# A linear attention with experts: the k times v products of a pair of heads formed on 32 columns of the array, behind the products of scores and v

## The chip, the cores and the metric

The kernel runs on one core of one Trainium2 chip. The metric is the time of one execution in microseconds (us) on the device; where a profile is shown, its span is the time from the first to the last instruction of the profiled execution. The engines are TensorE (PE, with the load of its stationary operand shown as PEld), VectorE (DVE), ScalarE (ACT), GpSimd (POOL) and SyncE (SP, which issues transfers here).

## The reference

The input x has 8 sequences of 1024 tokens with 256 features, all in fp32. A layer norm is followed by two branches whose results are added to x. The first is a causal linear attention with 16 heads of 16 features; the second sends each token to 2 of 8 experts.

```python
xn = layernorm(x)
# attention, per head (d, e run over 16 features)
q = elu(xn @ Wq.T) + 1;  k = elu(xn @ Wk.T) + 1;  v = xn @ Wv.T
kv_cumsum = cumsum(einsum('blhd,blhe->blhde', k, v), axis=1)
k_cumsum = cumsum(k, axis=1)
out = einsum('blhd,blhde->blhe', q, kv_cumsum)
out = out / clip(einsum('blhd,blhd->blh', q, k_cumsum), 1e-06, None)
attn = out @ Wo.T
# experts: the best 2 of 8, softmax over the two
h = silu(xn @ W1[e]) * (xn @ W3[e]);  y_e = h @ W2[e]
result = x + attn + sum(weight_e * y_e)
```

## The kernel before

The tokens are cut into 16 blocks of 512 (two per sequence), and a block into 4 chunks of 128, so there are 64 chunks. The experts' work is cut into tiles of 128 tokens that go to the same expert; 132 of them run. A loop over the expert tiles is the frame: each turn does one expert tile (`ffn_step`: two groups of 16 records gu, the gate and the up product, L1216; the turn of the next tile's tokens, L1183; the down product y of the tile before, L1235), and one or two steps of the attention are put between the turns by `attend_upto`. A block of the attention has nine steps: four for its projections (`project`), one for the scores of its first chunk, and four that weigh one chunk each. The instructions are not written out in their final order: a scheduler sets it on each engine, from the program's order, the dependencies and its own costs. From before to after it places the surrounding work anew.

The attention runs chunk by chunk. For a chunk, causality within it is taken by masked scores, and everything ahead of it by a state, one 16 x 16 matrix per head, which is the sum of k times v over all earlier chunks of the sequence.

- `scores(t, c)`: eight products (L919) on 32 rows of the array each, one row strip for each r, write q times k for 16 heads to four PSUM tiles `s_ps`, which are all four buffers of the pool `ps_mm`; the experts' products gu take their two from the same pool. VectorE multiplies each tile with the causal mask (L926) into `s_sb`, of the pool `masked` with seven buffers: four for the chunk that waits to be weighed, three for the next. Then two products (L934), one for each half of the 16 heads (`KC` = 2), form k times v: the stationary operand is 128 columns of k (8 heads), the moving one the 128 columns of v of these heads. Of the 128 x 128 result only the eight blocks of 16 x 16 on the diagonal are wanted; VectorE multiplies by a mask of them (`heads_b`, L939), and adds the state so far (L941), unless the chunk is the first of its sequence. The last chunk of a sequence needs no k times v.
- `weigh(t, c)`: two products of the state with q (L953; left out in the first chunk of a sequence), then sixteen of v and scores (L960) which each make 32 rows of the output on 32 columns of the array, all summed in the PSUM tile `o_ps`. VectorE multiplies with the reciprocal of the denominator (L967) to `oT`.
- `attend(t, c, oT)`: the two products with Wo (L979), copied by ScalarE and added to the output.

`block_steps` calls `scores` one chunk ahead of `weigh`, and `attend` one chunk behind it. Each fp32 product shows as two records in the trace: a group of 4 records is 2 products, 32 records are 16 products. The layout of v, `va`, holds pairs of heads: for each pair, one block of 32 columns with the first head's v and zeros, and one with zeros and the second's; `own_v` picks the filled 16 of each. `kv_ps`, `o_ps`, the turned tokens `xg_t` and the transposes `tp` share the pool `ps_t` with two buffers.

Of the kernel before, what the change touches and what calls it, by code (L numbers as in the profile page):

```python
# [46 lines left out]
F32 = mybir.dt.float32  # L47
# [3 lines left out]
ALU = mybir.AluOpType  # L51
AX = mybir.AxisListType

P = 128
# [3 lines left out]
PAIR = 2 * HD  # L58
# [5 lines left out]
def tile_attention_moe(  # L64
# [14 lines left out]
    nc = tc.nc  # L79
    B, L, H = x.shape  # L80
    E, _, I = w1.shape
    KC = H // P
    IC = I // P
    TB = 512
    NCH = TB // P
    N = B * L
    NBLK = N // TB
    BLK_PER_SEQ = L // TB
# [22 lines left out]
    three = ctx.enter_context(tc.tile_pool(name="three", bufs=3))  # L111
# [3 lines left out]
    ps_t = ctx.enter_context(tc.tile_pool(name="ps_t", bufs=2, space=bass.MemoryType.PSUM))  # L115
# [114 lines left out]
    heads = const.tile([P, P], F32, name="heads")  # L230
# [16 lines left out]
    va = const.tile([P, NCH, HALF, 2, PAIR], F32, name="va")  # L247
# [12 lines left out]
        nc.gpsimd.tensor_copy(own_of[:, o, o * HALF : (o + 1) * HALF], own)  # L260

    causal_b = causal.unsqueeze(1).to_broadcast([P, 4, P])
    heads_b = heads.unsqueeze(1).to_broadcast([P, KC, P])


    lgs = {}
# [116 lines left out]
    new = f_one.tile([P, E, MOST], F32, name="new")  # L383
# [384 lines left out]
    def own_v(va, c, a, b):  # L768

        pairs = va[:, c, a:b].rearrange("p g s d -> p g (s d)")  # L770
        return pairs.rearrange("p g (q d) -> p g q d", d=HD)[:, :, 0:4:3, :]
# [135 lines left out]
    state = [None]  # L907

    def scores(t, c):

        qT, qm, kT, kn, va, rden = blocks[t]
        first = t % BLK_PER_SEQ == 0 and c == 0
        last = t % BLK_PER_SEQ == BLK_PER_SEQ - 1 and c == NCH - 1
        span = bass.ts(c, P)
        s_ps = [ps_mm.tile([P, KC, 2, P], F32, tag="mm", name="s_ps") for r in range(4)]
        for hh in range(KC):
            for r in range(4):
                rows = slice(32 * r, 32 * r + 32)
                nc.tensor.matmul(  # L919
                    s_ps[r][:, hh].rearrange("p a l -> p (a l)"), lhsT=kT[rows, hh, span],  # L920
                    rhs=qm[rows, hh, :, span], start=True, stop=True,
                )
        s_sb = []
        for r in range(4):
            sm = masked.tile([P, KC * 2, P], F32, tag="s_sb", name="s_sb")
            nc.vector.tensor_tensor(  # L926
                sm, s_ps[r].rearrange("p k a l -> p (k a) l"), causal_b, ALU.mult
            )
            s_sb.append(sm)
        before_c = state[0]  # L930
        if not last:
            kv_ps = ps_t.tile([P, KC, P], F32, tag="t", name="kv_ps")
            for hh in range(KC):
                nc.tensor.matmul(  # L934
                    kv_ps[:, hh, :], lhsT=kn[:, c, bass.ts(hh, P)],
                    rhs=own_v(va, c, 4 * hh, 4 * hh + 4), start=True, stop=True,
                )
            new = three.tile([P, KC, P], F32, tag="kv", name="kv")
            nc.vector.tensor_tensor(new, kv_ps, heads_b, ALU.mult)  # L939
            if not first:  # L940
                nc.vector.tensor_tensor(new, new, before_c, ALU.add)  # L941
            state[0] = new
        return t, c, s_sb, before_c

    def weigh(t, c, s_sb, before_c):

        qT, qm, kT, kn, va, rden = blocks[t]
        first = t % BLK_PER_SEQ == 0 and c == 0
        span = bass.ts(c, P)
        o_ps = ps_t.tile([P, KC, P], F32, tag="t", name="o_ps")  # L950
        if not first:
            for hh in range(KC):
                nc.tensor.matmul(  # L953
                    o_ps[:, hh, :], lhsT=before_c[:, hh, :], rhs=qT[:, hh, span],
                    start=(hh == 0), stop=False, skip_group_check=True,
                )
        for hh in range(KC):
            for a in range(2):
                for r in range(4):
                    nc.tensor.matmul(  # L960
                        o_ps[32 * r : 32 * r + 32, hh, :],
                        lhsT=va[:, c, 4 * hh + r, a, :],
                        rhs=s_sb[r][:, 2 * hh + a, :],
                        start=(first and a == 0), stop=(a == 1), skip_group_check=True,
                    )
        oT = two.tile([P, KC, P], F32, tag="oT", name="oT")
        nc.vector.tensor_tensor(oT, rden[:, c], o_ps, ALU.mult)  # L967
        return oT

    ats = {}  # L970
# [24 lines left out]
    def block_steps(t):  # L995


        for i, _ in enumerate(project(t)):
            if i == 1 and behind:
                attend(*behind.pop())  # L1000
            if i in (1, 3, 5, 8):
                yield
        if t + 1 < NBLK:
            fetch(t + 1)
        waiting = scores(t, 0)
        yield
        done = None
        for c in range(NCH):
            coming = scores(t, c + 1) if c + 1 < NCH else None
            if done and c + 1 < NCH:  # L1010
                attend(*done)
            oT = weigh(*waiting)
            if done and c + 1 == NCH:
                attend(*done)
            done = t, c, oT
            waiting = coming
            if c + 1 < NCH or t + 1 < NBLK:
                yield
        behind.append(done)
        if t + 1 == NBLK:  # L1020
            attend(*behind.pop())
            yield
# [24 lines left out]
    with tc.manual_schedule(engines={EN.DVE, EN.Activation, EN.PE, EN.Pool}):  # L1047
# [63 lines left out]
        for _ in range(2):  # L1111
            idle_ps = ps_mm.tile([P, TB], F32, tag="mm", name="idle_ps")
            nc.tensor.matmul(
                idle_ps, lhsT=ident, rhs=blocks[0][0][:, 0, :], start=True, stop=True
# [170 lines left out]
    for j in range(NM + 1):  # L1285
        if j + 1 < NM:
            ffn_norm(j + 1)
        t = FB + j
# [27 lines left out]
        if LISTS <= j < LISTS + NBLK - FB:  # L1316
            t = FB + j - LISTS
# [66 lines left out]
```

## Time and profile before

| | |
|---|---|
| time, median of 3 runs | 1318.28 us (1317.63 to 1319.15) |
| the profiled execution: its time, its span | 1329.68 us, 1328.0 us |
| granted TensorE clock, mean | 0.989 |
| TensorE: gate and up products L1216 | 4224 records, 511.2 us busy |
| TensorE: down product L1235 | 1056 records, 250.6 us |
| TensorE: scores L919 | 1024 records, 85.5 us |
| TensorE: scores times v L960 | 2048 records, 73.2 us |
| TensorE: state times q L953 | 224 records, 34.9 us |
| VectorE: masked scores L926 | 256 instructions of 128x512, mean 684 ns |
| VectorE: k times v masked L939, state added L941 | 56 of mean 417 ns, 48 of mean 426 ns |
| VectorE: `oT` L967 | 64 of mean 414 ns |

A line of groups gives the source line, the engine, the operation, the tiles it writes and reads, the shapes and the count; then the busy time in us, the mean of one in ns, and the idle time of the engine ahead of it. A line of the timeline gives the start and the width in us, the engine, the source line and the count of instructions of that group which followed each other. A matmul's shape is given by its stationary operand (rows*columns) and its moving one.

### The profile page before, as it was taken

The page shows a single profiled execution, that of the slowest core. Times are in us where ns is not written, and L with a number is a line of the kernel's source. Part 1 is how long each engine was busy: PE and PEld are TensorE (multiplying, and loading weights), DVE is VectorE, ACT ScalarE, POOL GpSimd, SP SyncE. Part 2 cuts the span into 40 slices and gives each one's busy share as a digit, 9 for nine tenths or more (in the row PEclk, how much of TensorE's full clock was granted, in tenths as well). Part 3 has the DMA queues.
Part 4 walks back from the last instruction along what each step waited for, and adds up shares of the span by engine and source line. Part 5 has one row for each costly group of instructions (what it writes and reads, how often), then busy time and mean ns, then how long its engine had stood idle before and what let it go on. Part 6 is the DMA issues. An engine that isn't in the chain of part 4 may idle for free.

```text
span 1328.0 us, 28290 instructions
## 1 busy us (share of the span) xinstructions
PE 1270.6 (96%) x10968; PEld 1092.2 (82%) x10968; DVE 636.9 (48%) x1436; ACT 526.1 (40%) x1060; POOL 523.1 (39%) x460
## 2 busy tenths in 40 slices
PE   5689999999999999999999999999999999999996
PEld 4478887787888888888888888898888888888886
DVE  7667489764252434435343535344443525243441
ACT  4466364461524325161525243341515152433411
POOL 3633333233254443443443525343434334343432
PEclk9899999999999999999999999999999999999998
DMA  9688576466685766666675757476676767575763
GB/s 340 229 276 258 154 200 170 130 173 206 176 229 141 198 166 155 189 173 172 169 190 145 216 132 208 126 188 171 160 186 170 189 153 194 147 198 134 198 161 72
DMA packets 163462, 240.36 MB, mean 181 GB/s; under 512 B 16098, under 2 KB 87394, under 8 KB 163042
## 3 DMA queue, kind: packets, MB, share of 16 engines
q1 hardware_dynamic: 119938, 184.31, 45.0%
q0 software_dynamic: 38064, 43.22, 19.3%
q10 hardware_dynamic: 5328, 11.01, 2.3%
q8 instruction: 90, 1.47, 0.5%
q14 instruction: 42, 0.34, 0.1%
HBM read 196.30 MB, written 52.67 MB: 187 GB/s over the span
## 4 chain that ended last, share of the span: by engine, by line
PE 87%; DVE 7%; ACT 2%; issue 1%; DMA 1%; another core or an unknown queue 1%; POOL 0%; POOLq 0%; DVEq 0%; ACTq 0%
PE gu_ps L1216 34%; PE y_ps L1235 16%; PE o_ps L960 5%; PE s_ps L919 5%; PE a_ps L979 4%; PE zq L795 4%; PE zkk L811 4%; PE zkv L811 4%; PE kv_ps L934 2%; PE o_ps L953 2%; PE xg_t L1183 2%; DVE s_sb L926 1%; PE tp L333 1%; PE den L880 1%; PE tp L858 1%
## 5 line engine op out<-in xcount | busy, mean ns | idle before, releaser
L1216 PE MATMUL gu_ps<-xgT,w 128*128 128x128 f32 x4224 | 511.2, 278 | 8.9 <-DVE s_sb L926 7.6
L1216 PEld LDWEIGHTS gu_ps<-xgT,w 128*128 128x128 f32 x4224 | 492.5, 193 | 28.8 <-issue 12.5
L1162 POOL DMA_INDIRECT xg<-in_x_dram,src_i x132 | 128.1, 970 | 406.1 <-ACT xgT L1185 322.4
L1246 POOL DMA_INDIRECT out_dram<-y,dst_i x107 | 176.3, 1648 | 222.2 <-DVE kn L765 54.2
L1235 PE MATMUL y_ps<-w_sb,hT 128*128 x1056 | 250.6, 380 | 2.6 <-DVE hT L1227 2.0
L1227 DVE TENSOR_TENSOR hT<-gu_ps,hT 128x512 f32<-128x512 f32 x132 | 91.1, 690 | 274.4 <-PE gu_ps L1216 198.0
L1235 PEld LDWEIGHTS y_ps<-w_sb,hT 128*128 128x128 f32 x1056 | 190.2, 190 | 24.0 <-DVE hT L1227 1.9
L1224 ACT ACTIVATE hT<-gu_ps 128x512 f32<-128x512 f32 x132 | 78.8, 597 | 299.9 <-PE gu_ps L1216 255.0
L926 DVE TENSOR_TENSOR s_sb<-s_ps,causal 128x512 f32<-128x512 f32 x256 | 163.6, 684 | 54.0 <-PE s_ps L919 25.5
L1242 DVE TENSOR_SCALAR y<-y_ps,entry 128x256 f32<-128x256 f32 x132 | 63.5, 481 | 120.0 <-PE y_ps L1235 75.0
L1167 POOL DMA_INDIRECT entry<-tab_d,of_i x107 | 106.5, 995 | 32.6 <-issue 30.5
L1185 ACT COPY xgT<-xg_t 128x256 f32<-128x256 f32 x132 | 49.0, 371 | 145.2 <-PE xg_t L1183 141.7
L984 ACT COPY at<-a_ps 128x256 f32<-128x256 f32 x64 | 23.7, 370 | 159.2 <-PE a_ps L979 149.0
L919 PE MATMUL s_ps<-qm,kT 32*128 32x256 f32 x1024 | 85.5, 405 | 0.5 <-DVE hT L1227 0.4
L1174 ACT ACTIVATE xg<-xg,entry 128x256 f32<-128x256 f32 x132 | 79.6, 603 | 3.4 <-issue 3.4
L960 PE MATMUL o_ps<-s_sb,va 128*32 128x128 f32 x2048 | 73.2, 276 | 0.0
L919 PEld LDWEIGHTS s_ps<-qm,kT 32*128 32x128 f32 x1024 | 51.0, 184 | 24.2 <-issue 19.6
L979 PE MATMUL a_ps<-wo_sb,oT 128*128 128x256 f32 x256 | 69.0, 393 | 0.1
L1246 POOL DMA_INDIRECT acc_d<-y,src_i x25 | 44.0, 1761 | 55.2 <-DVE y L1242 15.4
L960 PEld LDWEIGHTS o_ps<-s_sb,va 128*32 128x32 f32 x2048 | 53.2, 109 | 9.8 <-DVE oT L967 0.8
L811 PE MATMUL zkk<-wkv_sb,xnT 128*128 128x256 f32 x256 | 60.0, 384 | 0.0
L795 PE MATMUL zq<-xnT,wq_sb 128*128 128x512 f32 x128 | 59.9, 609 | 0.0
(211 smaller groups left out, 1361.7 us busy)
## 6 DMA issues: line engine op xcount, KB each, us to landing
w<-in_w_dram SPq DMA_DIRECT2D x264, 512.0 KB
den_d<-over SPq DMA_DIRECT2D x64, 128.0 KB
rden<-den_d SPq DMA_DIRECT2D x16, 512.0 KB
xnT_d<-xnT ACTq DMA_DIRECT2D x15, 512.0 KB
xnT<-xnT_d SPq DMA_DIRECT2D x15, 512.0 KB
out_dram<-in_x_dram SPq DMA_DIRECT2D x12, 512.0 KB
out_dram<-at POOLq DMA_DIRECT2D x12, 512.0 KB
xb<-in_x_dram SPq DMA_DIRECT2D x10, 512.0 KB
```

The costliest lines, as they stand in the source:

```text
L795: nc.tensor.matmul(z, lhsT=wq_sb[:, k, bass.ts(o, P)], rhs=xnTs[t][:, k, :], start=(k == 0), stop=(k == KC - 1),)
L811: nc.tensor.matmul(z[:, i, :], lhsT=xnTs[t][:, k, bass.ts(c + i, P)], rhs=wkv_sb[:, k, a, :], start=(k == 0), stop=(k == KC - 1),)
L919: nc.tensor.matmul(s_ps[r][:, hh].rearrange("p a l -> p (a l)"), lhsT=kT[rows, hh, span], rhs=qm[rows, hh, :, span], start=True, stop=True,)
L926: nc.vector.tensor_tensor(sm, s_ps[r].rearrange("p k a l -> p (k a) l"), causal_b, ALU.mult)
L960: nc.tensor.matmul(o_ps[32 * r : 32 * r + 32, hh, :], lhsT=va[:, c, 4 * hh + r, a, :], rhs=s_sb[r][:, 2 * hh + a, :], start=(first and a = ...
L979: nc.tensor.matmul(a_ps, lhsT=oT[:, hh, :], rhs=wo_sb[:, hh, :], start=(hh == 0), stop=(hh == 1),)
L1162: nc.gpsimd.indirect_dma_start(out=xg[j], out_offset=None, in_=x_rows[:, :], in_offset=bass.IndirectOffsetOnAxis(ap=src_i[:, i : i + 1], a ...
L1167: nc.gpsimd.indirect_dma_start(out=entry[j], out_offset=None, in_=table[:, :], in_offset=bass.IndirectOffsetOnAxis(ap=num_i[:, i : i + 1], ...
L1216: done = nc.tensor.matmul(ps[:, i, :], lhsT=w13[:, k, bass.ts(i, P)], rhs=xgT[j][:, k, :], start=(k == 0), stop=(k == KC - 1),)
L1227: nc.vector.tensor_tensor(hT, gu[1], hT, ALU.mult)
L1235: done = nc.tensor.matmul(y_ps, lhsT=hT[:, i, :], rhs=w2_sb[:, bass.ds(e * (IC * H) + i * H, H)], start=(i == 0), stop=(i == IC - 1),)
L1246: nc.gpsimd.indirect_dma_start(out=rows[:, :], out_offset=bass.IndirectOffsetOnAxis(ap=dst_i[:, i : i + 1], axis=0), in_=ys.pop(j), in_off ...
```

## The change

The k times v products leave `scores` and go to the end of `weigh`, behind the products of scores and v. They are cut differently: instead of two products with 128 columns of k against 128 of v, there are eight, one for each pair of heads, with the 32 columns of k of the pair against its 32 of v, each on a strip of 32 columns of the array, so that four of them fill the array's width. The result of a strip lies on the 32 rows of the pair, and holds the 2 x 2 blocks of the pair only. So `kv_ps` has 2 x 32 columns instead of 2 x 128, and shares one PSUM tile with `o_ps`.

VectorE's multiply reads each group of 32 columns four times (a broadcast) against the same mask, and writes the state in its old form, 2 x 128 columns; the blocks of other pairs become zero. It and the add stand behind the multiply that makes `oT`. `weigh` reads the state ahead of its own products, as the chunk's state of before.

```diff
     def scores(t, c):
...
-        before_c = state[0]
-        if not last:
-            kv_ps = ps_t.tile([P, KC, P], F32, tag="t", name="kv_ps")
-            for hh in range(KC):
-                nc.tensor.matmul(
-                    kv_ps[:, hh, :], lhsT=kn[:, c, bass.ts(hh, P)],
-                    rhs=own_v(va, c, 4 * hh, 4 * hh + 4), start=True, stop=True,
-                )
-            new = three.tile([P, KC, P], F32, tag="kv", name="kv")
-            nc.vector.tensor_tensor(new, kv_ps, heads_b, ALU.mult)
-            if not first:
-                nc.vector.tensor_tensor(new, new, before_c, ALU.add)
-            state[0] = new
-        return t, c, s_sb, before_c
+        return t, c, s_sb
...
     def weigh(t, c, s_sb):
...
-        o_ps = ps_t.tile([P, KC, P], F32, tag="t", name="o_ps")
+        both_ps = ps_t.tile([P, KC * P + KC * PAIR], F32, tag="t", name="o_ps")
+        o_ps = both_ps[:, 0 : KC * P].rearrange("p (k l) -> p k l", k=KC)
+        kv_ps = both_ps[:, KC * P :].rearrange("p (k d) -> p k d", k=KC)
+        before_c = state[0]
...
+        if not last:
+            for hh in range(KC):
+                for r in range(4):
+                    nc.tensor.matmul(
+                        kv_ps[32 * r : 32 * r + 32, hh, :],
+                        lhsT=kn[:, c, hh * P + 32 * r : hh * P + 32 * r + 32],
+                        rhs=own_v(va, c, 4 * hh + r, 4 * hh + r + 1),
+                        start=True, stop=True, skip_group_check=True,
+                    )
         oT = two.tile([P, KC, P], F32, tag="oT", name="oT")
         nc.vector.tensor_tensor(oT, rden[:, c], o_ps, ALU.mult)
+        if not last:
+            new = three.tile([P, KC, P], F32, tag="kv", name="kv")
+            nc.vector.tensor_tensor(
+                new.rearrange("p k (g d) -> p k g d", d=PAIR),
+                kv_ps.unsqueeze(2).to_broadcast([P, KC, 4, PAIR]),
+                heads.rearrange("p (g d) -> p g d", d=PAIR).unsqueeze(1).to_broadcast(
+                    [P, KC, 4, PAIR]
+                ),
+                ALU.mult,
+            )
+            if not first:
+                nc.vector.tensor_tensor(new, new, before_c, ALU.add)
+            state[0] = new
         return oT
```

More of the change, by code (lines that the diff above doesn't have):

```diff
@@ L262, in tile_attention_moe @@
     causal_b = causal.unsqueeze(1).to_broadcast([P, 4, P])
-    heads_b = heads.unsqueeze(1).to_broadcast([P, KC, P])
     lgs = {}
@@ L911, in scores @@
         qT, qm, kT, kn, va, rden = blocks[t]
-        first = t % BLK_PER_SEQ == 0 and c == 0
-        last = t % BLK_PER_SEQ == BLK_PER_SEQ - 1 and c == NCH - 1
         span = bass.ts(c, P)
@@ L929, in scores, with weigh @@
             s_sb.append(sm)
-        before_c = state[0]
-        if not last:
-            kv_ps = ps_t.tile([P, KC, P], F32, tag="t", name="kv_ps")
-            for hh in range(KC):
-                nc.tensor.matmul(
-                    kv_ps[:, hh, :], lhsT=kn[:, c, bass.ts(hh, P)],
-                    rhs=own_v(va, c, 4 * hh, 4 * hh + 4), start=True, stop=True,
-                )
-            new = three.tile([P, KC, P], F32, tag="kv", name="kv")
-            nc.vector.tensor_tensor(new, kv_ps, heads_b, ALU.mult)
-            if not first:
-                nc.vector.tensor_tensor(new, new, before_c, ALU.add)
-            state[0] = new
-        return t, c, s_sb, before_c
-    def weigh(t, c, s_sb, before_c):
+        return t, c, s_sb
+    def weigh(t, c, s_sb):
         qT, qm, kT, kn, va, rden = blocks[t]
         first = t % BLK_PER_SEQ == 0 and c == 0
+        last = t % BLK_PER_SEQ == BLK_PER_SEQ - 1 and c == NCH - 1
         span = bass.ts(c, P)
-        o_ps = ps_t.tile([P, KC, P], F32, tag="t", name="o_ps")
+        both_ps = ps_t.tile([P, KC * P + KC * PAIR], F32, tag="t", name="o_ps")
+        o_ps = both_ps[:, 0 : KC * P].rearrange("p (k l) -> p k l", k=KC)
+        kv_ps = both_ps[:, KC * P :].rearrange("p (k d) -> p k d", k=KC)
+        before_c = state[0]
         if not first:
```

## The prediction

> **What bounds the kernel now.** I read the page's busy row first, then the chain that ended last, then the groups by line, then the timeline of TensorE's matmuls through a step of the attention.
>
> ```profile
> PE 1270.6 (96%) x10968; PEld 1092.2 (82%) x10968; DVE 636.9 (48%) x1436; ACT 526.1 (40%) x1060; POOL 523.1 (39%) x460
> ...
> PE 87%; DVE 7%; ACT 2%; issue 1%; DMA 1%; another core or an unknown queue 1%; POOL 0%; POOLq 0%; DVEq 0%; ACTq 0%
> ...
> L934 PE MATMUL kv_ps<-va,kn 128*128 128x128 f32 x224 | 40.0, 302 | 0.0
> ```
>
> TensorE is busy 96% of the 1328.0 us and carries 87% of the chain, so a microsecond off its queue is a microsecond off the end, except where it was going to wait anyway. Busy time of a short group overlaps its neighbours' pipeline tails (four records of 302 ns mean are 0.71 us wide, and the next group starts before that is over). So I price by start to start in the timeline:
>
> ```profile
> 751.51 1.15 PE L919 MATMUL s_ps<-qm,kT 32*128 32x256 f32 x16
> 752.59 0.71 PE L934 MATMUL kv_ps<-va,kn 128*128 128x128 f32 x4
> 753.23 1.08 PE L960 MATMUL o_ps<-s_sb,va 128*32 128x128 f32 x32
> 754.24 3.84 PE L1216 MATMUL gu_ps<-xgT,w 128*128 128x128 f32 x32
> ...
> 761.03 0.71 PE L934 MATMUL kv_ps<-va,kn 128*128 128x128 f32 x4
> 761.58 1.03 PE L979 MATMUL a_ps<-wo_sb,oT 128*128 128x256 f32 x4
> 762.45 0.61 PE L953 MATMUL o_ps<-qT,kv 128*128 128x128 f32 x4
> 762.99 1.08 PE L960 MATMUL o_ps<-s_sb,va 128*32 128x128 f32 x32
> 764.00 3.84 PE L1216 MATMUL gu_ps<-xgT,w 128*128 128x128 f32 x32
> ```
>
> Columns: start, width, engine, line. Read starts only. The v product (kv, 4 records) holds the queue 0.64 us ahead of L960 (752.59 to 753.23) and 0.55 us ahead of L979 (761.03 to 761.58); L979 takes 0.87, L953 0.54, the 32 records of L960 1.01, and the queue runs without a hole into the next gate product.
>
> ```profile
> 375.68 0.64 PE L880 MATMUL den<-ksum,own_of 128*32 128x128 f32 x16
> 376.25 1.36 PE L919 MATMUL s_ps<-qm,kT 32*128 32x256 f32 x16
> 377.54 0.71 PE L934 MATMUL kv_ps<-va,kn 128*128 128x128 f32 x4
> 379.49 3.84 PE L1216 MATMUL gu_ps<-xgT,w 128*128 128x128 f32 x32 [1.25 <-DVE s_sb L926]
> ```
>
> Here, at a block's first chunk, kv is followed by the gate product, and that waits 1.25 us for the eviction of the scores on VectorE (L926): all four `ps_mm` buffers hold scores. 16 records of den take 0.57 us, the 16 of the scores 1.29.
>
> **What the Trainium skill says.** "TensorEngine Tiling (Array Packing)", Key Properties: a change of the tiling mode drains TensorE. The trace agrees: L979 takes 0.87 after kv (full array to full array), and 0.96 straight after the scores (697.68 to 698.64, the last chunk of a sequence); kv ahead of L960 takes 0.64, ahead of L979 0.55. So about 0.10 us to enter and 0.09 to leave. "TensorE: Matmul & The Clock Gate", Part 3, says that column tiles run at the same time: 32 records of L960 against 16 of den make (1.01 - 0.57) / 16 = 27.5 ns each, where a full-array record with the same 128 moving columns takes 0.112 (32 in 3.57 us when nothing changes mode), so four do run together. The same page, LDWEIGHTS, prices a load at columns / 1.2 ns, 27 ns for 32 columns. The rows agree in slope: mean 109 ns for 32 columns (L960) and 193 for 128 (L934) is 84 ns for 96 columns. "PSUM — Partial Sum Buffer", PSUM bank collisions, asks that accesses of two engines be kept apart by bank and quadrant: in the changed program the multiply of `oT` waits for TensorE and the one that reads kv behind it has no TensorE wait of its own, so `oT` waits for the kv products too.
>
> **The change, part by part.** The program has 64 chunks, 56 with a kv product. Counts below are from the order of instructions of the two builds.
>
> *Removed: 56 full-array kv groups.* By what follows the group:
> - 22 times L979 follows: 0.55 + 0.87 now; then L979 comes straight after the scores at 0.96. Gain 0.45. 10 times L953 follows: 0.55 + 0.54 against 0.64 with an entry, gain 0.45. Together 32 x 0.45 = 14.4 us.
> - 8 times L960 follows (first chunk of a sequence): the scores go straight to column tiles, one drain where there were two. Gain 0.64 each, 5.1 us. The trace of before shows row tiles to column tiles almost nowhere; if the entry stays, 0.54 each, 4.3. I take 5.1.
> - 15 times the gate product follows, and once the turn L1183. In nearly all of the 15 TensorE then waits for VectorE's evictions, whose times the change does not touch: the 0.55 us only lay inside that wait. Gain 0 (if two or three had no wait, 1 us more).
>
> *Moved: the order of the last two chunks of a block.* Five times before has L960, L953, six records of L960, two of the gate, 26 of L960, L979, 30 of the gate: 700.19 to 706.91, 6.72 us and four mode changes past the first.
>
> ```profile
> 697.68 1.13 PE L979 MATMUL a_ps<-wo_sb,oT 128*128 128x256 f32 x4
> 698.64 0.61 PE L953 MATMUL o_ps<-qT,kv 128*128 128x128 f32 x4
> ...
> 700.19 0.71 PE L953 MATMUL o_ps<-qT,kv 128*128 128x128 f32 x4
> ...
> 706.91 0.38 PE L1183 MATMUL xg_t<-ident,xg 128*128 128x128 f32 x2
> ```
>
> In the changed program the L953 of the last chunk needs the state made by VectorE just then, and the scheduler puts ten gate records and L979 ahead of it: 10 x 0.112 + 0.10, 0.87, 0.54, 1.01, 22 x 0.112 + 0.10, or 6.20 us. Gain 0.5, five times: 2.5 us.
>
> *Added: 56 x 16 records of 128 x 32 weights and 32 moving columns*, behind L960 and in its mode, so no new drain; the exit that L960 paid is paid behind them. They go as four quads (four column groups at once, as L960's 32 records are eight quads of 0.109). The trace shows no quad this short. Above: if the quad kept L960's pace, 4 x 0.109 = 0.44 us, 24.4 in all. Below: the weight load, 27 ns by the skill's price (an estimate), 4 x 0.027 = 0.11, 6.0 in all; a quarter of L960's moving columns comes to 0.109 / 4, the same. Under "Instruction Overhead" the tiling page says that a matmul of one column takes as long as one of 60; if this holds for each of a record's passes, the quad is nearer 0.055, 12.3 in all. L960's own quads are long enough to be set by their moving columns, since a load slope of 27 ns fits four times into 109; so I take 0.035, or 0.14 us a chunk, 7.8 us.
>
> *VectorE.* The multiply (mean 417 ns) reads a quarter of the data, repeated, but still makes 256 columns: 0.42 again; the add 0.43 again. VectorE is 48% busy, so the sum there is unchanged. What changes is the place: before, multiply and add filled the time in which VectorE waited for L960 to free the seventh `masked` buffer (0.39 us at 764.18); now they stand behind the fourth eviction and `oT`, and in a block's second chunk behind the expert's y. Its queue there is y (0.48), `oT` (0.41), multiply, add, then the evictions of the next scores, and L979, queued behind the 1.08 us of the scores, waits for `oT`: 0.89 plus gaps against 1.08. L953 is 0.96 later and waits for the add: 1.74 plus gaps against 2.04. Both just fit. In the five regrouped pairs L979 waits for `oT`, some 1.3 to 1.6 us behind L960's end, with 0.14 + 1.22 of cover. I allow 2 us for such waits over the whole run, from 0 to 8. Losing that cover wholly is the second rival.
>
> *Nothing else.* SP's instructions stand in the same order, POOL's differ by one swap of two loads, ACT's order changes only where the lists are made (before 340 us), where TensorE had holes that the scheduler fills differently; I count this 0, within 3 us either way. One `ps_t` tile less per chunk can only free the turn.
>
> **Sum.** -14.4 - 5.1 - 2.5 + 7.8 + 2.0 = -12.2 us in the profiled execution, so a span of 1315.8. That execution took 1329.68 against a median of 1318.28 for the runs, 0.9% more, and the difference scaled is -12.1: 1306.
>
> **Rivals.**
> 1. *A small column tile costs what a large one does* (slower). If a quad keeps 0.109 us because a record's time is fixed and not its columns', the kv products cost 24.4 us: -22.0 + 24.4 + 2.0 = +4.4, some 1322. For it: no short quad is in the trace. Against it: score records with 256 moving columns pace at about 0.216 a quad and L960's with 128 at 0.109, so columns set the pace down to there. It decides from (22.0 - 2.0) / 224 = 0.089 us a quad.
> 2. *VectorE's queue takes the place of the kv products*: in each of 16 blocks the chain y, `oT`, multiply, add, evictions makes L979, L953 or the gate product late by 0.3 to 0.6 us, 5 to 10 us. For it: the two margins of 0.2 and 0.3 us. Against: in the middle of a block VectorE rests 2.7 us ahead of hT. -12.2 + 8 gives 1314.
> 3. *The floor of a small matmul is twice what I take*, 0.055 to 0.08 a quad: +4 to +10, 1310 to 1316. It adds to the forecast without ending it.
> 4. *The change does not do what it says*: two accumulation groups lie in one bank; were they kept apart by a wait on TensorE itself, 56 pipeline tails of about 0.2 us, 11 us, would take the gain. TensorE's kv products follow L960 with no wait between, so I give this little.
>
> **How the numbers follow.** Forecast (0.027 to 0.05 a quad, stalls 0 to 4): 0.68, with its own range 1301 to 1310. Rival 1: 0.10. Rival 2: 0.10. Rival 3: 0.09. Rival 4: 0.03. The range that holds 8 in 10 runs from 1299 (the lowest quad, no stall, 3 us from the early part) to 1315 (rivals 2 and 3 in great part). A change under 0.2% (2.6 us) can't be told from none here; that is above 1315.6. Faster: 0.68, and most of rivals 2 and 3, 0.83. Same: 0.06. Slower: rival 1 and a part of rival 4, 0.11.
>
> **What would show it.** TensorE's busy time falls by some 12 us with 672 more records (896 added, 224 gone). The timeline of a middle step goes from the scores to L979 at once, L979 takes 0.96, and from the first kv record to the gate product it is about 0.1 to 0.2 us longer than L960's 1.01 alone accounted for. In the first chunk of a block the gate product starts as long after the scores as before. Wrong it would be if the new group held 0.3 us or more, or if L979 or L953 show idle time for `oT` or kv in most blocks.

## The result, and the profile after

The changed kernel takes 1300.88 us (median of 4 runs, 1299.69 to 1302.3) against 1318.72 for the kernel before on the same chip: 0.9859 of it, 95% interval 0.9845 to 0.9873, or 17.8 us less. The forecast was 1306.0 with a range of 1299 to 1315. The gain is of the kind that was forecast, and larger than the forecast 12.1 by 5.7 us; the times are 5.1 apart, as the kernel before took 0.4 more here than in the runs that the forecast was scaled to.

The profiled execution took 1299.69 us with a span of 1298.0, at a mean granted clock of 0.992. Its page, engines and chain:

```profile
PE 1241.2 (96%) x11640; PEld 1078.2 (83%) x11640; DVE 635.1 (49%) x1436; ACT 526.1 (41%) x1060; POOL 526.6 (41%) x460
...
PE 88%; DVE 7%; DMA 2%; issue 1%; ACT 1%; POOL 1%; POOLq 0%; DVEq 0%; ACTq 0%
```

TensorE has 672 more records and 29.4 us less busy time than before (1270.6 in both profiled executions of the kernel before), and is still 96% busy. That busy time fell by more than the run did comes with the overlap of widths that the prediction warned of: a group's width includes its pipeline tail. So again only starts are read. TensorE's timeline of the changed kernel, two steps of a block's attention with the regrouped pair in the second:

```profile
750.02 1.15 PE L916 MATMUL s_ps<-qm,kT 32*128 32x256 f32 x16
751.09 1.13 PE L990 MATMUL a_ps<-wo_sb,oT 128*128 128x256 f32 x4
752.06 0.61 PE L941 MATMUL o_ps<-qT,kv 128*128 128x128 f32 x4
752.60 1.08 PE L948 MATMUL o_ps<-s_sb,va 128*32 128x128 f32 x32
753.50 0.31 PE L958 MATMUL o_ps<-va,kn 128*32 128x32 f32 x16
753.73 1.38 PE L1227 MATMUL gu_ps<-xgT,w 128*128 128x128 f32 x10
754.95 1.03 PE L990 MATMUL a_ps<-wo_sb,oT 128*128 128x256 f32 x4
755.82 0.61 PE L941 MATMUL o_ps<-qT,kv 128*128 128x128 f32 x4
756.35 1.08 PE L948 MATMUL o_ps<-s_sb,va 128*32 128x128 f32 x32
757.25 0.31 PE L958 MATMUL o_ps<-va,kn 128*32 128x32 f32 x16
757.49 2.72 PE L1227 MATMUL gu_ps<-xgT,w 128*128 128x128 f32 x22
```

The lines have moved: L990 was L979, L941 was L953, L948 was L960, L958 is the new group, L1227 was L1216. The scores go straight to L990, which takes 0.97 us (751.09 to 752.06). L948 and the new group take 1.13 us together (752.60 to 753.73) where L960 alone took 1.01: 16 small records cost 0.12 us of the queue. The gate product then begins without a hole.

At a block's first chunk:

```profile
935.81 1.36 PE L916 MATMUL s_ps<-qm,kT 32*128 32x256 f32 x16
937.82 3.84 PE L1227 MATMUL gu_ps<-xgT,w 128*128 128x128 f32 x32 [0.66 <-DVE s_sb L923]
```

Here the k times v products are gone from between the scores and the gate product, and that waits in their place: 2.01 us from one to the other. In the execution that the prediction used, the kernel before took 3.24 at such a place. In a second execution of it (the first experiment below) it takes 2.01 too, so nothing was gained there:

```profile
373.19 1.36 PE L919 MATMUL s_ps<-qm,kT 32*128 32x256 f32 x16
...
375.20 3.84 PE L1216 MATMUL gu_ps<-xgT,w 128*128 128x128 f32 x32
```

Where the time came from is best counted by steps. A step runs from the first record of one down product (y) to the first of the next, and holds one expert tile and what of the attention was put beside it. From the 27th expert tile on, where the order of work repeats block by block, a second execution of each kernel (below) gives these lengths. Steps with the same order of groups repeat to within 0.01 us:

| attention's groups in the step | steps | before, us | after, us | together |
|---|---|---|---|---|
| scores, L979, L953, L960 and kv | 17 | 9.75 | 9.43 | -5.5 |
| scores, L953, L960 and kv | 7 | 8.89 | 8.57 | -2.3 |
| scores, L960 and kv (first chunk of a sequence) | 6 | 8.44 | 7.93 | -3.1 |
| the five regrouped pairs, sum | 5 | 63.49 | 60.86 | -2.6 |
| scores, then the gate product (first chunk of a block) | 5 and 8 | 7.64 and 11.76 | 7.64 and 11.76 | 0 |
| steps that have kv only after the change, of three kinds | 4, 2, 2 | 9.31, 8.03, 12.33 | 9.43, 8.16, 12.45 | +1.0 |
| all others (projections, turns, experts alone) | | | unchanged to 0.01 each | 0 |

The sum is -12.5 us, for 45 of the 56 chunks with a kv product. The rest of the gain lies ahead of the 27th tile, with the other 11 chunks, and at the very end.

### The profile page after: what moved, and what is told of

Read it like the earlier page. It is cut to its first block, busy times and chain, and to the rows that moved or that the text cites. A ratio compares the mean times of both kernels' runs of the same rounds, so it can differ in the third digit from the quotient of the medians.

```text
span 1298.0 us, 29674 instructions
## 1 busy us (share of the span) xinstructions
PE 1241.2 (96%) x11640; PEld 1078.2 (83%) x11640; DVE 635.1 (49%) x1436; ACT 526.1 (41%) x1060; POOL 526.6 (41%) x460
## 4 chain that ended last, share of the span: by engine, by line
PE 88%; DVE 7%; DMA 2%; issue 1%; ACT 1%; POOL 1%; POOLq 0%; DVEq 0%; ACTq 0%
PE gu_ps L1227 36%; PE y_ps L1246 16%; PE o_ps L948 5%; PE a_ps L990 5%; PE s_ps L916 4%; PE zq L794 4%; PE zkk L810 4%; PE zkv L810 4%; PE xg_t L1194 2%; PE o_ps L941 2%; DMA xb<-in_x_dram 1%; PE tp L857 1%; PE tp L332 1%; DVE at_place L572 1%; DVE s_sb L923 1%
## 5 line engine op out<-in xcount | busy, mean ns | idle before, releaser
L1227 PE MATMUL gu_ps<-xgT,w 128*128 128x128 f32 x4224 | 510.5, 278 | 14.2 <-DVE s_sb L923 9.3
L1227 PEld LDWEIGHTS gu_ps<-xgT,w 128*128 128x128 f32 x4224 | 490.8, 193 | 30.7 <-DVE s_sb L923 13.8
L1257 POOL DMA_INDIRECT out_dram<-y,dst_i x107 | 179.4, 1677 | 214.1 <-issue 50.6
L1253 DVE TENSOR_SCALAR y<-y_ps,entry 128x256 f32<-128x256 f32 x132 | 63.5, 481 | 121.3 <-PE y_ps L1246 121.2
L990 PE MATMUL a_ps<-wo_sb,oT 128*128 128x256 f32 x256 | 70.9, 400 | 2.2 <-DVE oT L965 2.2
L948 PE MATMUL o_ps<-s_sb,va 128*32 128x128 f32 x2048 | 70.7, 276 | 0.0
L990 PEld LDWEIGHTS a_ps<-wo_sb,oT 128*128 128x128 f32 x256 | 45.2, 192 | 24.0 <-issue 14.8
L948 PEld LDWEIGHTS o_ps<-s_sb,va 128*32 128x32 f32 x2048 | 52.5, 110 | 10.0 <-issue 2.2
```

The source lines that it names most:

```text
L948: nc.tensor.matmul(o_ps[32 * r : 32 * r + 32, hh, :], lhsT=va[:, c, 4 * hh + r, a, :], rhs=s_sb[r][:, 2 * hh + a, :], start=(first and a = ...
L990: nc.tensor.matmul(a_ps, lhsT=oT[:, hh, :], rhs=wo_sb[:, hh, :], start=(hh == 0), stop=(hh == 1),)
L1227: done = nc.tensor.matmul(ps[:, i, :], lhsT=w13[:, k, bass.ts(i, P)], rhs=xgT[j][:, k, :], start=(k == 0), stop=(k == KC - 1),)
L1257: nc.gpsimd.indirect_dma_start(out=rows[:, :], out_offset=bass.IndirectOffsetOnAxis(ap=dst_i[:, i : i + 1], axis=0), in_=ys.pop(j), in_off ...
```

## The experiments

My theory (A) was that the change works through TensorE's queue alone: mode changes saved, small column tiles nearly free, VectorE just in time. Against it stood that one of the two parts, cut or place, does the whole (B), and that stalls or chance account for a part.

**The kernel before, once more.** No edit. The profile that the prediction rested on was of an execution 0.9% above the median.

> The kernel before, unchanged, for a second profile. Its profiled execution took 1329.68 us against a median of 1318.7, and in five of its blocks the step over (L886) started 0.6 to 0.9 us later after den than in the others, so that the gate product behind the first scores waited up to 1.5 us instead of 0.2 to 0.3. Theory A (chance of that one execution): span near 1317, and in nearly all blocks over starts 0.34 us after the last record of den, and from the first kv record to the gate product it takes 0.73 or 0.88. Theory B (a property of the kernel before, which the change took away): the five late starts are there again, in the same blocks, and 4.4 us of the gain are theirs.

Measured: 1321.98 us in one execution, span 1320.3 and so not near 1317. But VectorE's maximum of the denominator, the start of the chain at a block's first chunk, began 0.34 us behind the last record of den in 14 of 16 blocks. In the first profile it had begun up to 1.25 us behind it in those 14, so that wait of 1.25 us which the prediction showed was partly chance of that execution; all 13 such steps of this one are as long as after the change. It is the execution to compare with, and is the "before" of the table above.

**The place alone**: two full-width products, but behind L960.

```diff
             for hh in range(KC):
-                for r in range(4):
-                    nc.tensor.matmul(
-                        kv_ps[32 * r : 32 * r + 32, hh, :],
-                        lhsT=kn[:, c, hh * P + 32 * r : hh * P + 32 * r + 32],
-                        rhs=own_v(va, c, 4 * hh + r, 4 * hh + r + 1), ...
+                nc.tensor.matmul(
+                    kv_ps[:, hh, :], lhsT=kn[:, c, bass.ts(hh, P)],
+                    rhs=own_v(va, c, 4 * hh, 4 * hh + 4), ...
...
```

The PSUM tile and VectorE's multiply take the full width again with them.

> The full-width kv products of before (2 of 128 x 128), moved behind the products of scores and v. Theory A (the gain is the price of the small products; the place alone gives nothing): a group of 4 full records with an entry is 0.55 us where the four quads of the changed kernel and the later entry into full-array mode took 0.12 + 0.10, so 56 x 0.32 = 18 us more than the changed kernel, some 1319, as before. Theory B (the place and the new order around it are the gain): within 5 us of the changed kernel, under 1306.

Measured: 1319.75 us (12 runs), 0.9993 of before, interval 0.9981 to 1.0005: no difference. Its steps say why: 9.75 and 8.89, as before. The end of a middle step:

```profile
971.62 0.71 PE L958 MATMUL o_ps<-va,kn 128*128 128x128 f32 x4
972.16 3.74 PE L1219 MATMUL gu_ps<-xgT,w 128*128 128x128 f32 x32
```

The full-width products still hold the queue for 0.54 us. In the order of groups, the change to the full array that the gate product made behind L960 is now made by them, and the one that they made behind the scores is made by the product with Wo (0.97 us instead of 0.87); the number of mode changes is the same. The sequence's first chunks gain (8.25 for 8.44, 1.2 us in six), and so do the five regrouped pairs together (63.1 for 63.5). Against that, the 8 steps that have a kv product only after the move are 0.45 us longer each, 3.6 us: the kv products of a block's first chunk left the wait in which they had cost nothing. So no difference in time is here a sum of gains and losses.

**The cut alone**: eight small products, but at their old place behind the scores.

```diff
     def scores(t, c):
...
-                nc.tensor.matmul(
-                    kv_ps[:, hh, :], lhsT=kn[:, c, bass.ts(hh, P)], ...
+                for r in range(4):
+                    nc.tensor.matmul(
+                        kv_ps[32 * r : 32 * r + 32, hh, :],
+                        lhsT=kn[:, c, hh * P + 32 * r : hh * P + 32 * r + 32], ...
```

> The eight small kv products at the old place, behind the scores. Theory A: ahead of L979 or L953 they take about 0.24 (four quads of 0.031, and a drain) and leave the entry into the full array to the next group, 0.21 less than before, 32 times: 6.6 us; ahead of L960 they need no drain of their own, 0.5 less, 8 times: 4 us; ahead of the gate product nothing. 1318.7 - 10.7 = 1308. Theory B (the place is the gain): within 3 us of before.

Measured: 1309.32 us (4 runs), 0.9913, interval 0.9892 to 0.9933. TensorE's timeline of it, a middle step:

```profile
961.20 1.15 PE L919 MATMUL s_ps<-qm,kT 32*128 32x256 f32 x16
962.28 0.33 PE L935 MATMUL kv_ps<-va,kn 128*32 128x32 f32 x16
962.54 1.13 PE L989 MATMUL a_ps<-wo_sb,oT 128*128 128x256 f32 x4
```

Between the scores and L989 the same 16 records take 0.26 us (962.28 to 962.54) and not 0.12. The order there has one change of mode more, from row tiles to column tiles and then to the full array instead of straight to the full array, and it costs some 0.14 us; behind L948 it is not there. The step is 9.57 us, so of the 0.32 gained in a middle step the cut gives 0.18 and the place, once the products are cut, 0.14. At a sequence's first chunk, where column tiles follow the scores in any case, the cut alone gives the whole gain (7.93 us, as after the change). So the cut alone gives more than half of the gain, the place alone nothing, and the place pays only once the products are cut.

**The small products twice, and four times.** The later sets write the same values again, so these kernels do more work and compute the same.

```diff
-            for hh in range(KC):
+            for hh in list(range(KC)) * 2:      # four times: * 4
                 for r in range(4):
                     nc.tensor.matmul(
                         kv_ps[32 * r : 32 * r + 32, hh, :],
```

> The changed kernel with each small kv product made twice into the same place, which doubles the added group and nothing else. Theory A (a quad takes 0.031 us and lies on the path): 56 x 4 x 0.031 = 6.9 us more than the changed kernel, 1307.8. Theory B (the small products lie in time that TensorE lost anyway, as between modes): within 2 us of 1300.9. Theory C (a quad costs as much as one of the products of scores and v, 0.109): 24 us more.

Measured: 1315.14 us (13 runs), 0.9962, interval 0.9949 to 0.9976, between A and C. The steps of the middle grew from 9.43 to 9.63, so the second set costs 0.20 us where the first cost 0.12. In the order of records, the first seven quads began 0.031 us apart; behind the 25th record there was a gap of 0.031, and then the records came one by one, mostly 0.016 to 0.018 apart. I took that for a supply that had run dry, and asked the next run.

> The changed kernel with its small k times v products made four times over (the later sets write the same values again). Twice, they cost 0.197 us a chunk for the second set and not the 0.124 of the first; in the trace the matmul records began every 8 ns at first and every 16 to 18 ns from about the 57th record behind the start of the products of scores and v. Theory A (small records are held to some 16 ns each once a store of some 57 has run dry): each further set is 16 records x 16.5 ns = 0.26 us, so 2 x 56 x 0.26 = 29 us more than with two sets, 1344 us, and the third and fourth set as long as each other. Rival B (the second set's price was chance or had to do with writing the same place twice; a set is 0.124): 14 us more, 1329. Rival C (every set but the first costs 0.197): 22 us more, 1337.

Measured: 1336.82 us (4 runs), 1.0135, interval 1.0111 to 1.0159. The total is rival C's, but the trace is not:

```profile
983.27 1.08 PE L948 MATMUL o_ps<-s_sb,va 128*32 128x128 f32 x32
984.17 0.77 PE L958 MATMUL o_ps<-va,kn 128*32 128x32 f32 x64
984.87 3.84 PE L1227 MATMUL gu_ps<-xgT,w 128*128 128x128 f32 x32
```

64 records take 0.70 us in most chunks, so the third and fourth set cost (0.70 - 0.43) / 2 = 0.13 each, as the first did. My theory of a supply that lasts for some 57 records falls: there is one surplus of 0.07 us that begins behind the 25th small record, paid once, and behind it four records take 0.033 us again. What that surplus is stays open. The two traces are 20.4 us apart. From the 27th tile on the records of kv account for 14.2 us of that (including some chunks of up to 1.06 us); 6.4 us arose ahead of it, where every one of these programs is laid out anew.

**The changed kernel once more, with three others on the same chip.**

> The changed kernel once more, unchanged, beside the three others of this call. If the stretch before the 26th expert tile was shortened by the change itself, it begins that tile within 1.5 us of 331.9 us from the span's start, where the four other programs began it at 337.6 to 341.4. If that was chance of one execution, it begins it at 336 or later. Time 1301 either way if most of the runs had it, up to 1305 if not.

Measured: 1302.15 us (5 runs), 0.9863, interval 0.9843 to 0.9884. Its 26th tile began at 334.8 us: neither within 1.5 of 331.9 nor at 336. The two executions of before began it at 344.5 and 341.4. So the stretch ahead of it differs by about 3 us from one execution to the next of the same program, and is shorter by 7 to 13 us after the change, where its 11 chunks account for 2.5 by the prices found.

The traces show where. The 3 us between executions of one program have arisen by the 17th down product (249.6 and 246.3 us before, 242.7 and 245.5 after). From there to the 25th the two executions of before take 91.9 and 92.2 us and those of the changed kernel 86.4 both, so this part of the difference repeats. Of it 3.7 to 3.9 us lie in the turn between the 20th and the 21st down product, in which TensorE also makes the denominator (den). The gate product of that turn and what follows it, first in the second execution of before, then in that of the changed kernel:

```profile
286.62 5.47 PE L1216 MATMUL gu_ps<-xgT,w 128*128 128x128 f32 x32
291.92 3.62 PE L811 MATMUL zkv<-wkv_sb,xnT 128*128 128x256 f32 x16
```

```profile
285.15 3.84 PE L1227 MATMUL gu_ps<-xgT,w 128*128 128x128 f32 x32
288.83 3.62 PE L810 MATMUL zkv<-wkv_sb,xnT 128*128 128x256 f32 x16
```

The same 32 records take 5.30 us and 3.68 (4.85 and 3.68 in the first executions). The granted clock over this turn was 0.90 in both executions of before and 1.00 in both of the changed kernel, and the two waits of den for VectorE came to 2.20 us before and to 1.36 and 1.40 after. So between these traces 2.0 to 2.4 us come from this turn's waits and its clock, and not from the prices of the queue. They do not belong to the small products as such: in two versions of the changed kernel that follow (oT last, first chunk early) this gate product took over 5 us again, and with the place alone and with the products twice it took 3.7. Which difference in the order of the work brings them is not shown, nor why the clock was lower. From the 27th tile on the two executions of the changed kernel agree to 0.6 us.

**Is VectorE really just in time?** The prediction saw margins of 0.2 and 0.3 us for oT and the state and allowed 2 us for stalls; from the 27th tile on none appeared. The chain of VectorE in the changed kernel, where a block's second chunk has oT behind the expert's y, and the products that wait for it on TensorE:

```profile
952.22 0.48 DVE L1253 TENSOR_SCALAR y<-y_ps,entry 128x256 f32<-128x256 f32 x1 [1.19 <-PE y_ps L1246]
952.62 0.41 DVE L965 TENSOR_TENSOR oT<-rden,o_ps 128x256 f32<-128x256 f32 x1
952.94 0.42 DVE L968 TENSOR_TENSOR kv<-o_ps,heads 128x256 f32<-128x256 f32 x1
```

```profile
952.11 1.15 PE L916 MATMUL s_ps<-qm,kT 32*128 32x256 f32 x16
953.18 1.13 PE L990 MATMUL a_ps<-wo_sb,oT 128*128 128x256 f32 x4
```

oT ends at 952.62 + 0.41 = 953.03, and L990 starts 0.15 us later, at its earliest behind the scores. The smallest such gap, where L990 did wait, is 0.06, so 0.1 us is to spare, in 8 places; in 6 more, at the regrouped pairs, it is under 0.2. Two experiments tried to use it up. The first put oT behind the state's multiply and add:

```diff
-        oT = two.tile([P, KC, P], F32, tag="oT", name="oT")
-        nc.vector.tensor_tensor(oT, rden[:, c], o_ps, ALU.mult)
         if not last:
             new = three.tile([P, KC, P], F32, tag="kv", name="kv")
...
             state[0] = new
+        oT = two.tile([P, KC, P], F32, tag="oT", name="oT")
+        nc.vector.tensor_tensor(oT, rden[:, c], o_ps, ALU.mult)
         return oT
```

> The changed kernel with VectorE's multiply oT put behind the multiply and the add of the state, so oT comes 0.85 us later; VectorE's work and TensorE's are the same, but for five pairs where the order of TensorE becomes six gate records, L990's first half, L941, L948, kv, L990's second half. In the trace of the changed kernel L990 starts 0.16 us behind the end of oT in 8 places and 0.24 in 6, and where it did wait 0.06 behind it. Theory A (these small margins are real, and the change just kept within them): L990 late by 0.85 - 0.10 = 0.75 in 8 places, 6.0 us, and by 0.85 - 0.18 - 0.11 = 0.56 in 6, 3.4, and the split of L990 about 0.2 in 5, 1.0: 10.4 us, 1311. Rival B (what hides oT is larger than the records show, or TensorE makes it up in a wait behind): 1301 to 1303.

Measured: 1302.98 us (6 runs), 0.988, interval 0.9859 to 0.9901: B's number, for a reason of neither theory. In those 8 places the scheduler put the multiply and the add ahead of y, into time in which VectorE rested, and oT came no later than before; elsewhere it put oT between multiply and add, in 13 middle steps 0.33 us later with a margin of over 5. L990 was not late, and the run says nothing of the margin. The second delays oT by work that depends on it:

```diff
         nc.vector.tensor_tensor(oT, rden[:, c], o_ps, ALU.mult)
+        for _ in range(2):
+            nc.vector.tensor_tensor(
+                oT, oT, ones[:, 0:1].unsqueeze(1).to_broadcast([P, KC, P]), ALU.mult
+            )
```

> The run with oT put last did not move oT in the 8 places where it stands behind the expert's y: the scheduler put the state's multiply and add ahead of y there. Here the changed kernel multiplies oT twice more by one, in place, so its value is the same and it can't be ready early. TensorE's order in the middle of a block is the same; VectorE's in those 8 places is y, oT, multiply, first pass, add where there is one, second pass, evictions, each some 0.33 us behind the one before. Theory A (the margins of 0.16 us in the trace, 0.10 of them to spare, are what keeps L990 on time): L990 late by 3 x 0.33 - 0.10 = 0.9 us in 4 places and by 4 x 0.33 - 0.10 = 1.2 in 4, 8.4 us, and up to 2 from the five pairs, where the scheduler now puts L941, L948 and kv ahead of L990: 1309 to 1313. Rival B (there is more cover than the margins show): 1301 to 1303.

Measured: 1314.41 us (19 runs), 0.9963, interval 0.9953 to 0.9973. A little above A's range, and its mechanism is plain in TensorE's waits, where the columns are the total, the times and the longest:

```profile
PE a_ps L994 <- DVE oT L967: 8.5, 8, 1.2
```

In the same view of the changed kernel this wait is one of 2.2 us, early in the run. In the timeline of the run with passes, at the place shown above:

```profile
962.12 1.15 PE L916 MATMUL s_ps<-qm,kT 32*128 32x256 f32 x16
964.43 1.13 PE L994 MATMUL a_ps<-wo_sb,oT 128*128 128x256 f32 x4 [1.16 <-DVE oT L967]
```

L994 starts 2.31 us behind the scores and not 1.07. Eight such steps take 10.45 to 10.67 us and 13 others with the same groups 9.43: the delay costs where the margin was 0.1 us, and nothing where it was over 5. Against the changed kernel's second execution the run is 9.2 us longer from the 27th tile on, and 2.6 us up to it.

**A version with less on the path.** At a block's first chunk the gate product waits about 0.7 us anyway. Its kv products go there, behind the scores, with a PSUM tile of their own:

```diff
             s_sb.append(sm)
-        return t, c, s_sb
+        early = None
+        if c == 0:
+            early = ps_t.tile([P, KC, PAIR], F32, tag="t", name="kv_ps")
+            products(early, kn, va, c)      # the eight small products
+        return t, c, s_sb, early
...
```

> The changed kernel with the small k times v products of each block's first chunk put behind its scores, into the 0.73 to 0.88 us for which the gate product waits there for VectorE, into a tile of their own; the others stay behind the products of scores and v. Theory A (what lies in that wait is free): 16 x 0.124 = 2.0 us less, 1299. Rival B (the wait is not free, as the small products bring a change of mode in front of the gate product, or the additional tile of PSUM delays a turn): 1301 or more.

Measured: 1301.55 us (5 runs), 0.9868, interval 0.9847 to 0.989; against 1302.15 for the changed kernel beside it, that is less than the runs can tell apart. TensorE's timeline:

```profile
936.32 1.36 PE L916 MATMUL s_ps<-qm,kT 32*128 32x256 f32 x16
937.60 0.33 PE L936 MATMUL kv_ps<-va,kn 128*32 128x32 f32 x16
938.33 3.84 PE L1236 MATMUL gu_ps<-xgT,w 128*128 128x128 f32 x32 [0.40 <-DVE s_sb L923]
```

The gate product starts 2.01 us behind the scores, as without the products, and the steps with the sequel fell from 8.57 to 8.44 and from 7.93 to 7.80: 1.6 us over 13 blocks, as theory A had it. In the trace the version is the better one; in the time this isn't shown.

## Why the prediction was right, and where 5 us were missed

*Removed, ahead of L979 and L953: 0.45 each.* The step fell by 0.32, and the new group in it costs 0.124, so 0.45 was freed. Right.

*Removed, ahead of L960: 0.64 each.* 0.52 + 0.124 = 0.64. Right, with one drain and not two: the choice of 5.1 over 4.3 held.

*Removed, ahead of the gate product: nothing.* The 13 steps are equal to 0.01 us. Right.

*The regrouped pairs: 0.5 each.* Two kv groups less (0.45 each) and seven small ones more (0.124 each) cancel but for 0.02, so the 2.63 us are the regrouping alone: 0.53 each. Right.

*Added: 0.035 a quad, 0.14 a chunk.* Measured 0.031 and 0.124 (L948 and the new group take 1.135 together, L960 alone took 1.011). Over 56 chunks this is 0.9 us less than priced. Of the anchors the price of the weight load, an estimate of 27 ns by the section LDWEIGHTS of the Trainium skill's page "TensorE: Matmul & The Clock Gate", was the nearest; a quarter of the time of L960's moving columns gives the same 27, so which of the two sets the pace isn't shown. The 0.055 came from taking the minimum that the skill's page "TensorEngine Tiling (Array Packing)" states under Instruction Overhead once for each pass; read so, it does not show for these records. Rivals 1 and 3 fall by this number, and rival 4 with them: no wait stands between the two groups.

*VectorE: 2 us allowed for stalls.* From the 27th tile on none came. One wait of TensorE for oT, 2.2 us, stands in the early stretch of both traces of the changed kernel; in the same turn of both traces of before TensorE waits 1.3 us for the state. It is part of what the early stretch gave in sum. Rival 2 did not occur, but its reasoning was right: with 0.9 to 1.2 us more on that chain L990 is late in just the 8 places that have the margin of 0.1 us.

*Before 340 us: 0 within 3.* By the medians, the 5.7 us between the forecast's gain of 12.1 and the 17.8 measured are 2 allowed for stalls, 0.9 of the quads, and 2.8 that are left for the early stretch and the end. The last lie within the 3 that were allowed. The turn found above, with its shorter waits and its higher granted clock, is large enough for them; how much of it the usual execution has can't be told from two traces of each kernel. The low end of the range, 1299, was worked out from just this case: the lowest quad, no stall, and 3 us from the early part. That the early part helped and did not hurt was luck.

So no step failed in kind. The terms mis-sized were the allowance for stalls, the early stretch and, by 0.9 us, the quads, all to the same side. TensorE's busy time fell by 29.4 us and not by "some 12": that check compared widths, which the same text had said not to add.

## What to carry to other kernels

On a kernel that TensorE bounds, count the changes of tiling mode in the queue as well as the work of each product: here eight small products cost 0.12 us beside others of their own mode and 0.26 elsewhere, and neither the cut nor the place alone gave what both gave. Price such a move in steps that repeat, start to start, and take the counts from the order of instructions; from the 27th tile on the prices worked out beforehand give 26 x 0.45 + 6 x 0.64 + 2.5 - 45 x 0.14 = 11.7 us, and the steps gave 12.5. And when such a step leaves another engine just in time, measure the margin: here, with 0.1 us to spare in 8 places, two more short instructions on that chain brought 8.5 us of waits, half of the gain.

## What was not expected

- A column tile of 32 columns with 32 moving ones takes 0.031 us for four records, 7.8 ns for each record, and 0.033 in the later part of a run of 64. In between there is one surplus of 0.07 us, behind the 25th record, whose cause is open.
- One change of mode more, from row tiles (the scores) to column tiles ahead of the full array, costs some 0.14 us (0.26 against 0.12 for the same 16 records).
- Two executions of one program gave the stretch before the 26th expert tile 3 us apart, and the first profile of before had late starts on VectorE at the head of several blocks which the second did not have. In one turn of the early stretch the granted clock was 0.90 in both traces of before and 1.00 in both of the changed kernel, and the same 32 records took 5.30 and 3.68 us in the second trace of each. One profile is not enough to price waits of this size.
